# A graph network's attention decoder: one run of steps over all parts, with tanh, arguments and exponentials in one order, and sums in six tiles of one bank

## The chip, the cores and the metric

The kernel runs on one core of a Trainium2 chip. The metric is the device time of one execution, in microseconds (us); the time of a kernel is the median over its runs. The engines are named as the profile names them: PE is TensorE (its weight loads are PEld), DVE is VectorE, ACT is ScalarE, POOL is GpSimd, SP is SyncE, which here only issues transfers. Each engine works through its own list of instructions in order, and waits on semaphores for the others.

## The reference

Four graph layers over the same 2708 nodes with 512 features, each followed by a residual sum and a layer norm. Only the first matters here: an attention encoder, an mlp, and a decoder that uses the same attention again.

```python
sig = sigmoid(f1[:, :, None] + f2[:, None, :])         # heads x nodes x nodes
local_att = masked_softmax(local_pattern * sig, mask)  # both patterns are adj here
long_att = masked_softmax(long_range_pattern * sig, mask)
att = 0.5 * long_att + 0.5 * local_att
Xa = einsum('hij,hjd->hid', att, Xw)                   # encoder, 4 heads of 128
emb = mlp_block(batchnorm(Xa), ...)                    # h = elu(x W + b) + x, batchnorm
Y = einsum('hij,hjd->hid', att, emb by heads)          # decoder: the same attention
Y = elu(einsum('hnd,hed->hne', Y, W))
out = mlp_block(Y, ...)
x = layernorm(x + out)
```

The other layers are a mean over neighbours, and two attention layers with softmax over full score matrices. The change doesn't touch them.

## The kernel before

The decoder needs the exponentials of the attention again and has no room to keep them, so it forms most of them anew. Its sums are cut into four **parts**: half of the destination nodes (`hf`, 1354 columns each, in three chunks of at most 452) times a pair of heads (`p`). The order of the parts (`PARTS`) is (0,0), (0,1), (1,0), (1,1). A part has 22 **steps**, one for each block of 128 source nodes in `ORDER`; the block of the last 20 nodes, the remnant, stands at place 11. So there are 88 steps, in the text S0 to S87.

A step is either formed or kept. A **formed** step (`form`, L625) loads a block of the masked adjacency (`a`, 677 KB, SP's queue, three buffers), makes two tanhs on ACT, one for each head of the pair (`tanhs`, L383), multiplies with the mask on DVE (`arguments`, L378), and takes the exponential of both heads at once on ACT (L635). All of it works in place in a tile `t` of 128 x 2 x 1354 numbers, of which there are four buffers. DVE also counts each block's neighbours (`count`, L615), once for each half of the nodes: with the first formed step that has the block in hand. In a **kept** step, `t` is loaded back from DRAM (1354 KB), where the encoder wrote it: places 8, 11, 14 and 18 of the parts with p = 0, and places 1, 4, 7, 9, 11, 14, 17 and 20 of those with p = 1 (`KEPT`); the remnant at place 11 is kept in all four. Of the 88 steps 64 are formed and 24 kept.

Then come the **sums** (`feature_sums`, L640, matmul at L650): for the two heads and three chunks one matmul each into one of six PSUM sums `po`, which last for the whole part. The profile records each as two, so a full step has 12 records. The six sums lie in three tiles of two banks (`po0` to `po2`), used again by each part.

At the end of a part, `decode` (L1036) takes the sums: six times `take` (L1054, DVE) multiplies one sum with a scale and with the softmax's reciprocal sums `rb` into `ot`. Then, for each of the six, `shifted` (L1067, DVE), and `turn`: a matmul with the head's weights into `ps_y` (L1079) and elu (L699 on ACT, L706 and L708 on DVE). After the parts with p = 1 the decoder's mlp follows (`ps_dec`, L1093, elu at L701). This work isn't done at once: `decode` returns it as a list, `later`, and one piece is popped at each step of the next part (`later.pop(0)()`). The last part's is written out in `decode` itself. `rb` (L355, two loads of 677 KB) and a mask `linked` (L1041, DVE) are made at a part's start.

The order on an engine is that in which the program issues, unless a scheduler finds by its own estimates that another is better; `tc.issue_after(x)`, here wrapped as `behind(x)`, tells it that what is issued inside must stand behind x. Before, the decoder has only one such order for its work: a count stands behind its step's arguments. The rest, which tanh stands ahead of which exponential, is the scheduler's choice.

Ahead of the decoder stands the encoder's mlp (L954 to L985), in six chunks of nodes: four matmul groups of a chunk (`ps_mlp`, L964) into the same PSUM tiles `po0` to `po2`, two groups to a tile, elu, a sum and statistics on DVE, then transposes of the finished blocks (`tp_emb`, L983) and their copies to `emb` on ACT (L984). The decoder's first tanhs are made beside it.

The functions that the change touches:

Of the kernel before, what the change touches and what calls it, by code (L numbers as in the profile page):

```python
# [8 lines left out]
F32 = mybir.dt.float32  # L9
# [3 lines left out]
AF = mybir.ActivationFunctionType  # L13
# [4 lines left out]
P = 128  # L18
# [11 lines left out]
def gnn_stack_kernel(  # L30
# [25 lines left out]
    nc = tc.nc  # L56
    N, F = x.shape
    H = w0.shape[1]
    C = F // P
    NT = (N + P - 1) // P  # L60
    NFULL = N // P
    BLOCKS = [(i * P, min(P, N - i * P)) for i in range(NT)]
    BANK = 512


    Q = 32
# [71 lines left out]
    NHALF, HB, HP = 2, 3, 2  # L138
    HW = 2 * ((N + 3) // 4)
# [24 lines left out]
    ORDER = list(range(NT // 2)) + [NT - 1] + list(range(NT // 2, NT - 1))  # L164
# [5 lines left out]
    KEPT = [(8, 11, 14, 18), (1, 4, 7, 9, 11, 14, 17, 20)]  # L170
    KEPT = [[ORDER[k] for k in places] for places in KEPT]
# [17 lines left out]
    with ExitStack() as l0:  # L189
# [39 lines left out]
        def behind(*which):  # L229
            stack = ExitStack()  # L230
            for work in which:
                stack.enter_context(tc.issue_after(work.ins))
            return stack
# [116 lines left out]
        def spread_sums(att, hf, p):  # L350

            h0, w = HSPAN[hf]
            t = att.tile([P, HP, HW], F32, tag="rb", name="rb", bufs=1)
            for k in range(HP):
                nc.sync.dma_start(  # L355
                    t[:, k, :w], rs_d[HP * p + k, h0 : h0 + w].partition_broadcast(P)
                )
            return t
# [17 lines left out]
        def arguments(t, a, n, w):  # L376
            ab = a[:n, :w].unsqueeze(1).to_broadcast([n, HP, w])
            return nc.vector.scalar_tensor_tensor(t, t, GUARD, ab, ALU.add, ALU.mult)  # L378

        def tanhs(t, f1b, hf, p, jt, n, w):  # L380
            for k in range(HP):
                h = HP * p + k
                done = nc.scalar.activation(  # L383
                    t[:, k, :],
                    f1b[k][:n, :w],
                    AF.Tanh,
                    bias=f2h[:n, jt, h : h + 1],
                    scale=0.5,
                )
            return done  # L390
# [214 lines left out]
        def decoder_pass(values, att, psum, finish):  # L605

            def count(hf, jt, att, a=None):

                h0, w = HSPAN[hf]
                j0, n = BLOCKS[jt]  # L610
                if a is None:
                    a = att.tile([P, HW], F32, tag="a", name="a", bufs=3)
                    nc.sync.dma_start(a[:n, :w], adj_d[j0 : j0 + n, h0 : h0 + w])
                z = att.tile([P, HW], U8, tag="z", name="z", bufs=1)
                nc.vector.tensor_scalar(  # L615
                    z[:n, :w],
                    a[:n, :w],
                    -0.5 * BIG,
                    None,
                    ALU.is_lt,  # L620
                    ALU.add,
                    accum_out=zeros[:n, jt, hf : hf + 1],
                )

            def form(hf, p, jt, att, f1b, t, rows):  # L625

                h0, w = HSPAN[hf]
                j0, n = BLOCKS[jt]
                a = att.tile([P, HW], F32, tag="a", name="a", bufs=3)
                loads.append(nc.sync.dma_start(a[:n, :w], adj_d[j0 : j0 + n, h0 : h0 + w]))  # L630
                if n < P:
                    load_few(a, adj_d, h0, w)
                tanhs(t, f1b, hf, p, jt, rows, w)
                step = arguments(t, a, rows, w)
                nc.scalar.activation(t, t, AF.Exp, scale=0.5)  # L635
                if p == (jt in KEPT[0]):

                    with tc.issue_after(step.ins):
                        count(hf, jt, att, a)

            def feature_sums(part, place, t):

                hf, p = part
                jt = ORDER[place]
                n = BLOCKS[jt][1]
                for k in range(HP):
                    h = HP * p + k
                    for q, (q0, qw) in enumerate(HCH[hf]):
                        r = 0 if n == P else q * Q
                        nc.tensor.matmul(  # L650
                            po[HB * k + q][:, :qw],
                            values[r : r + n, jt, h * P : (h + 1) * P],
                            t[r : r + n, k, q0 : q0 + qw],
                            start=(place == 0),
                            stop=(place == NT - 1),
                        )

            later, loads = [], []
            for part in PARTS:
                hf, p = part  # L660
                h0, w = HSPAN[hf]
                for place, jt in enumerate(ORDER):
                    n = BLOCKS[jt][1]
                    if place == 0:
                        f1 = f1_d[HP * p : HP * (p + 1), h0 : h0 + w].partition_broadcast(P)
                        both = att.tile([P, HP, HW], F32, tag="f1b", name="f1b", bufs=2)
                        f1b = [both[:, k, :] for k in range(HP)]
                        with behind(*loads[-9:-8]):
                            nc.sync.dma_start(both[:, :, :w], f1)
                        rb = spread_sums(att, hf, p)  # L670
                    elif later:
                        later.pop(0)()
                    t = att.tile([P, HP, HW], F32, tag="t", name="t", bufs=4)
                    kept = kept_d.get((hf, p, jt))
                    if kept is None:
                        rows = n if n == P else HR
                        form(hf, p, jt, att, f1b, t[:rows, :, :w], rows)
                    else:
                        for r in range(0, P if n == P else HB * Q, P if n == P else Q):
                            nc.sync.dma_start(t[r : r + n, :, :w], kept[:n, :, :w])  # L680
                        if p == 0 and jt in KEPT[1]:
                            count(hf, jt, att)
                    if place == 0:
                        both = [
                            psum.tile([P, HP, BANK], F32, tag=f"po{q}", name="po", bufs=1)
                            for q in range(HB)
                        ]
                        po = [both[q][:, k, :] for k in range(HP) for q in range(HB)]
                    feature_sums(part, place, t)
                later += finish(hf, p, po, rb) or []  # L690
            for work in later:
                work()

# [216 lines left out]
        with (  # L910
# [43 lines left out]
            for ci, (c0, w) in enumerate(CHUNKS):  # L954
                if ci + 1 < NCH:
                    normal(ci + 1)
                pss = []
                for o in range(C):
                    if o % HP == 0:
                        slot = (C * ci + o) // HP % HB  # L960
                        pair = psum.tile([P, HP, BANK], F32, tag=f"po{slot}", name="ps_mlp")
                    ps = pair[:, o % HP, :]
                    for c in range(C):
                        nc.tensor.matmul(  # L964
                            ps[:, :w],
                            enc_w[:, c, o * P : (o + 1) * P],
                            ft[:, c, c0 : c0 + w],
                            start=(c == 0),
                            stop=(c == C - 1),
                        )  # L970
                    pss.append(ps)
                for o in range(C):
                    dst = ft[:, o, c0 : c0 + w]
                    r = elu(
                        att, pss[o][:, :w], w, prm_sb[:, MB_ENC, o : o + 1], less[:, o : o + 1]
                    )
                    nc.vector.tensor_tensor(dst, dst, r, ALU.add)
                    nc.vector.bn_stats(stats[:, o, ci, :], dst)
                while turned < NT and sum(BLOCKS[turned]) <= c0 + w:
                    j0, n = BLOCKS[turned]  # L980
                    tp = psum.tile([P, C, P], F32, tag="misc", name="tp_emb", bufs=2)
                    for c in range(C):
                        nc.tensor.transpose(tp[:n, c, :], ft[:, c, j0 : j0 + n], ident)  # L983
                    nc.scalar.copy(emb[:n, turned, :], tp[:n].rearrange("p c d -> p (c d)"))  # L984
                    turned += 1  # L985
# [1291 lines left out]
```

## Time and profile before

| what | value |
|---|---|
| median of three runs | 3121.74 us (3119.06 to 3122.14) |
| the profiled execution | 3120.7 us |
| its span in the trace, mean granted clock | 3118.8 us, 0.997 |
| busy: PE, DVE, ACT, POOL | 3070.6, 2025.3, 1353.1, 175.2 us |
| the decoder's sums, from first to last record | 589.57 to 1028.07 us |
| parts of the decoder, by the windows view | 590 to 695, 695 to 796, 796 to 905, 905 to 1028 us |
| encoder's mlp, PE busy in 505 to 590 | 83.35 us |
| after the decoder's sums, 1028 to 1176, PE busy | 145.87 us |

A time in the trace counts from the span's start. "Idle before" is the time for which an engine stood still just ahead of an instruction or a group of them, with the instruction that ended it ("<-ACT t L635"). Matmuls are pipelined: the end of a record is modelled, and within a run of matmuls it lies 0.17 us after the start of the next. The granted clock is a share of TensorE's full speed. All shares of busy time over the whole span mix four layers; what a change of the decoder is worth can only be read from its own windows.

### The profile page before, as it was taken

Reading aid. Unit: us, or ns where it says so; the run is one execution under the profiler, and the core shown is the slowest. Engines: PE = TensorE matmul, PEld = TensorE weight load, DVE = VectorE, ACT = ScalarE, POOL = GpSimd, SP = SyncE. Lnnn points to the kernel's source line nnn. Section 1 sums busy time; section 2 is a strip of 40 time slices with the busy share of each in tenths; the row PEclk is TensorE's granted clock in tenths of the full one; section 3 lists DMA queues with packets and bytes.
Section 4 is the critical chain, followed back from the end, with each engine's and each line's share of the span. In section 5 each row is a group of like instructions: output and inputs, shape, how many; then the busy total and the mean of one; then the engine's idle time right before and its main releaser. Section 6 shows DMA issues by size and latency. Waiting matters only on the chain.

```text
span 3118.8 us, 39610 instructions
## 1 busy us (share of the span) xinstructions
PE 3070.6 (98%) x15144; PEld 2336.9 (75%) x15144; DVE 2025.3 (65%) x3804; ACT 1353.1 (43%) x1655; POOL 175.2 (6%) x301
## 2 busy tenths in 40 slices
PE   8999999999999999999999999999999999999999
PEld 7999996544444447875588887787778888888886
DVE  7988966785885783452366668677555555555565
ACT  7999998587767350001133334435211111111111
POOL 1111100000000000000111101000010000000000
PEclk9999999999999999999999999999999999999999
DMA  8987964266445315530254445566331111111110
GB/s 277 333 313 251 321 235 144 79 232 221 161 173 192 108 42 158 144 97 31 67 166 133 136 138 165 164 177 184 108 95 36 50 51 51 51 51 50 50 52 29
DMA packets 207228, 430.10 MB, mean 138 GB/s; under 512 B 22218, under 2 KB 137598, under 8 KB 201294
## 3 DMA queue, kind: packets, MB, share of 16 engines
q1 hardware_dynamic: 182774, 326.20, 34.0%
q0 software_dynamic: 24256, 101.35, 8.9%
q8 instruction: 119, 1.95, 0.3%
q14 instruction: 71, 0.58, 0.1%
q10 hardware_dynamic: 8, 0.02, 0.0%
HBM read 330.07 MB, written 95.87 MB: 137 GB/s over the span
## 4 chain that ended last, share of the span: by engine, by line
PE 79%; ACT 8%; DVE 8%; issue 3%; DMA 1%; SPq 0%; DVEq 0%; ACTq 0%; POOLq 0%
PE po L1728 21%; PE ps_s L1523 18%; PE po L650 9%; PE ps_nb L1326 7%; PE ps_wide L1376 5%; PE po L548 4%; ACT t L383 4%; ACT t L515 3%; DVE t L378 2%; PE ps_v L131 2%; PE ps_sup L1934 2%; PE ps_hid L131 2%; PE ps_dec L1093 2%; PE ps_mlp L964 1%; DVE a L444 1%
## 5 line engine op out<-in xcount | busy, mean ns | idle before, releaser
L378 DVE SCALAR_TENSOR_TENSOR t<-t,a 128x2708 f32<-128x2708 f32 (+1 forms) x152 | 443.8, 2922 | 166.1 <-ACT t L383 165.8
L548 PE MATMUL po<-xw,t 128*128 128x129 f32 (+2 forms) x3872 | 428.2, 277 | 11.8 <-DVE rc L781 4.9
L548 PEld LDWEIGHTS po<-xw,t 128*128 128x128 f32 (+2 forms) x3872 | 422.8, 189 | 16.4 <-issue 7.9
L383 ACT ACTIVATE t<-f1b,f2h 128x1354 f32<-128x1354 f32 x296 | 404.4, 1412 | 34.2 <-PE po L650 34.2
L1523 PE MATMUL ps_s<-q,hT 128*128 128x256 f32 (+1 forms) x1848 | 405.5, 372 | 0.0
L1728 PE MATMUL po<-sup,e 128*128 128x256 f32 (+1 forms) x1512 | 398.2, 384 | 5.6 <-DVE c L1809 2.8
L650 PE MATMUL po<-t,emb 128*128 128x452 f32 (+3 forms) x1056 | 399.1, 547 | 4.3 <-ACT t L635 4.2
L1523 PEld LDWEIGHTS ps_s<-q,hT 128*128 128x128 f32 x1848 | 339.5, 190 | 49.5 <-issue 5.1
L650 PEld LDWEIGHTS po<-t,emb 128*128 128x128 f32 (+1 forms) x1056 | 194.2, 191 | 202.1 <-issue 189.2
L1728 PEld LDWEIGHTS po<-sup,e 128*128 128x128 f32 (+1 forms) x1512 | 264.7, 185 | 59.6 <-issue 19.8
L1728 PE MATMUL po<-held,T 128*128 128x256 f32 x1200 | 293.8, 380 | 0.0
L1728 PEld LDWEIGHTS po<-held,T 128*128 128x128 f32 x1200 | 227.0, 190 | 31.1 <-issue 0.9
L2129 DVE SCALAR_TENSOR_TENSOR e<-a_cols,ps_s 128x512 f32<-128x512 f32 (+1 forms) x121 | 79.6, 658 | 233.8 <-PE ps_s L1523 229.9
L1523 PE MATMUL ps_s<-hT 128*128 128x256 f32 (+2 forms) x968 | 213.8, 372 | 0.8 <-ACT sup L1941 0.7
L515 ACT ACTIVATE t<-t 128x2708 f32<-128x2708 f32 x88 | 209.2, 2377 | 8.8 <-DVE t L378 8.1
L1523 PEld LDWEIGHTS ps_s<-hT 128*128 128x128 f32 x968 | 175.1, 190 | 29.1 <-issue 3.9
L1326 PE MATMUL ps_nb<-hid_hi,at 128*128 128x512 f32 x484 | 185.6, 390 | 0.4 <-DVE at L1318 0.4
L635 ACT ACTIVATE t<-t 128x2708 f32<-128x2708 f32 x64 | 157.3, 2458 | 60.4 <-DVE t L378 60.2
L1326 PE MATMUL ps_nb<-hid_lo,at 128*128 128x512 f32 x462 | 180.0, 390 | 0.0
L2031 ACT ACTIVATE a_score<-a_score,neg_big 128x512 f32<-128x512 f32 (+3 forms) x131 | 88.4, 683 | 196.0 <-DMA a_score<-in_adjT_dram 98.9
L2121 ACT ACTIVATE q<-ps_wide,uq 128x256 f32<-128x256 f32 (+1 forms) x44 | 20.5, 465 | 335.7 <-PE ps_wide L1376 335.7
L1633 ACT ACTIVATE e<-e 128x512 f32<-128x512 f32 (+1 forms) x187 | 113.8, 615 | 118.2 <-DVE e L1632 117.9
(276 smaller groups left out, 3995.4 us busy)
## 6 DMA issues: line engine op xcount, KB each, us to landing
a<-adj_d SPq DMA_DIRECT2D x113, 677.0 KB
a_cols<-in_adjT_dram SPq DMA_DIRECT2D x200, 256.0 KB
kept<-t POOLq DMA_DIRECT2D x20, 1354.0 KB, 8.4
t<-kept SPq DMA_DIRECT2D x20, 1354.0 KB
raw<-in_adjT_dram SPq DMA_DIRECT2D x105, 256.0 KB
a<-in_adjT_dram SPq DMA_DIRECT2D x37, 677.0 KB
adj_d<-a POOLq DMA_DIRECT2D x37, 677.0 KB, 6.2
a_score<-in_adjT_dram SPq DMA_DIRECT2D x55, 256.0 KB
```

The costliest lines, as they stand in the source:

```text
L131: nc.tensor.matmul(ps[:n], xt[:, c, :n], w[:, c, :], start=(c == 0), stop=(c == C - 1))
L378: return nc.vector.scalar_tensor_tensor(t, t, GUARD, ab, ALU.add, ALU.mult)
L383: done = nc.scalar.activation(t[:, k, :], f1b[k][:n, :w], AF.Tanh, bias=f2h[:n, jt, h : h + 1], scale=0.5,)
L515: nc.scalar.activation(t, t, AF.Exp, scale=0.5)
L548: nc.tensor.matmul(po[k][b][:m, s * DR : (s + 1) * DR], t[own : own + n, k, i0 : i0 + m], values[own : own + n, jt, HP * p + k, :], start= ...
L635: nc.scalar.activation(t, t, AF.Exp, scale=0.5)
L650: nc.tensor.matmul(po[HB * k + q][:, :qw], values[r : r + n, jt, h * P : (h + 1) * P], t[r : r + n, k, q0 : q0 + qw], start=(place == 0), ...
L1326: nc.tensor.matmul(pos[it][:n], at, half[:, jt, :], start=(jt == 0 and k == 0), stop=(jt == NT - 1),)
L1376: nc.tensor.matmul(ps[:, :width], w(c, o), xt(c), start=(c == 0), stop=(c == C - 1),)
L1523: nc.tensor.matmul(ps[:, jb, i:w], keys[:, c, j : j + P], st["q"][:, c, i:], start=(c == 0), stop=(c == C - 1),)
L1633: return nc.scalar.activation(e, e, AF.Exp)
L1728: nc.tensor.matmul(po[bank][rows, half, :], lhsT, rhs, start=(k == 0 and half == 0) if first is None else first, stop=last, skip_group_che ...
```

## The change

Nothing is added to the work: each engine gets the same instructions as before, in another order, from the encoder's mlp on. Four things change.

1. The loop over parts and places becomes one loop over the 88 steps, in which `prepare(k)` runs two steps (`AFTER`) ahead of the sums: a part's first steps are prepared before the part ahead of it has issued its last sums and its `decode`.
2. Explicit orders: a step's tanhs stand behind the last exponential issued; its arguments behind the last arguments; the exponential of a formed step is issued only when the next formed step has issued its tanhs, and stands behind them; a count stands behind its step's arguments. So ACT gets tanh and exponential strictly in turn, over the kept steps too.
3. The six sums get a tile of one bank each, `po0` to `po5`, and so does `ps_mlp` in the encoder's mlp.
4. `rb` is loaded where a part's first sums are issued, behind the loads of `a` that were prepared ahead.

```diff
-            def form(hf, p, jt, att, f1b, t, rows):
+            def begin(hf, p, jt, f1b, t, rows):
...
                 loads.append(nc.sync.dma_start(a[:n, :w], adj_d[j0 : j0 + n, h0 : h0 + w]))
...
-                tanhs(t, f1b, hf, p, jt, rows, w)
-                step = arguments(t, a, rows, w)
-                nc.scalar.activation(t, t, AF.Exp, scale=0.5)
+                with behind(*exps[-1:]):
+                    tanh = tanhs(t, f1b, hf, p, jt, rows, w)
+                with behind(*args[-1:]):
+                    args.append(arguments(t, a, rows, w))
+                if open_exps:
+                    end(tanh)
+                open_exps.append(t)
                 if p == (jt in KEPT[0]):
-                    with tc.issue_after(step.ins):
+                    with behind(args[-1]):
                         count(hf, jt, att, a)
+
+            def end(*after):
+                t = open_exps.pop()
+                with behind(*after):
+                    exps.append(nc.scalar.activation(t, t, AF.Exp, scale=0.5))
...
-            for part in PARTS:
-                for place, jt in enumerate(ORDER):
...
+            AFTER = 2
+            def prepare(k):
+                (hf, p), place = STEPS[k]
...
+            state = {}
+            for k in range(len(STEPS) + AFTER):
+                if k < len(STEPS):
+                    prepare(k)
+                elif open_exps:
+                    end()
+                if k < AFTER:
+                    continue
+                part, place = STEPS[k - AFTER]
+                if place == 0:
+                    rb = spread_sums(att, *part)
+                    po = [
+                        psum.tile([P, BANK], F32, tag=f"po{b}", name="po", bufs=1)
+                        for b in range(HP * HB)
+                    ]
+                elif later:
+                    later.pop(0)()
+                feature_sums(part, place, tiles[k - AFTER])
+                if place == NT - 1:
+                    later += finish(*part, po, rb) or []
```

and in the encoder's mlp:

```diff
-                    if o % HP == 0:
-                        slot = (C * ci + o) // HP % HB
-                        pair = psum.tile([P, HP, BANK], F32, tag=f"po{slot}", name="ps_mlp")
-                    ps = pair[:, o % HP, :]
+                    slot = (C * ci + o) % (HP * HB)
+                    ps = psum.tile([P, BANK], F32, tag=f"po{slot}", name="ps_mlp")
```

More of the change, by code (lines that the diff above doesn't have):

```diff
@@ L656, in feature_sums @@
                         )
-            later, loads = [], []
-            for part in PARTS:
-                hf, p = part
+            later, loads, args, exps, open_exps, tiles = ([] for _ in range(6))
+            AFTER = 2
+            def prepare(k):
+                (hf, p), place = STEPS[k]
                 h0, w = HSPAN[hf]
-                for place, jt in enumerate(ORDER):
[L663 to L690, printed above, removed]
@@ new lines, in prepare @@
+                jt = ORDER[place]
+                n = BLOCKS[jt][1]
+                if place == 0:
+                    f1 = f1_d[HP * p : HP * (p + 1), h0 : h0 + w].partition_broadcast(P)
+                    f1b = att.tile([P, HP, HW], F32, tag="f1b", name="f1b", bufs=2)
+                    with behind(*loads[-9:-8]):
+                        nc.sync.dma_start(f1b[:, :, :w], f1)
+                    state["f1b"] = [f1b[:, i, :] for i in range(HP)]
+                t = att.tile([P, HP, HW], F32, tag="t", name="t", bufs=4)
@@ new lines, in prepare @@
+                kept = kept_d.get((hf, p, jt))
+                tiles.append(t)
+                if kept is None:
+                    rows = n if n == P else HR
+                    begin(hf, p, jt, state["f1b"], t[:rows, :, :w], rows)
+                    return
+                for r in range(0, P if n == P else HB * Q, P if n == P else Q):
+                    nc.sync.dma_start(t[r : r + n, :, :w], kept[:n, :, :w])
+                if p == 0 and jt in KEPT[1]:
+                    count(hf, jt, att)
@@ new lines, in decoder_pass @@
+            state = {}
[7 more added lines that the diff above has]
+                part, place = STEPS[k - AFTER]
+                if place == 0:
+                    rb = spread_sums(att, *part)
[8 more added lines that the diff above has]
+                    later += finish(*part, po, rb) or []
```

## The prediction, made before the changed kernel had run

> **What bounds it now.** I read the page's groups first, for the three lines of the decoder that the change reorders (line, engine, tiles, count, busy us, mean ns, then idle ahead of them and its releaser):
>
> ```profile
> L383 ACT ACTIVATE t<-f1b,f2h 128x1354 f32<-128x1354 f32 x296 | 404.4, 1412 | 34.2 <-PE po L650 34.2
> L650 PE MATMUL po<-t,emb 128*128 128x452 f32 (+3 forms) x1056 | 399.1, 547 | 4.3 <-ACT t L635 4.2
> L635 ACT ACTIVATE t<-t 128x2708 f32<-128x2708 f32 x64 | 157.3, 2458 | 60.4 <-DVE t L378 60.2
> ```
>
> ACT stood idle for 60 us ahead of the exponentials, but PE's sums lost 4.3 us in the whole decoder. Next the windows view over the decoder's four parts (PE, PEld, DVE, ACT, POOL busy, granted clock):
>
> ```profile
> 590.00:695.00 105.00, 104.03 (x291) 51.46 (x290) 79.38 (x71) 86.98 (x59) 1.56 (x3) 1.00 0.58 192
> ...
> 796.00:905.00 109.00, 108.53 (x285) 53.68 (x286) 95.89 (x101) 75.48 (x56) 0.00 (x0) 0.97 0.49 166
> 905.00:1028.00 123.00, 123.00 (x332) 61.05 (x331) 70.19 (x56) 85.36 (x54) 0.00 (x0) 1.00 0.49 175
> ```
>
> **PE bounds the decoder**: in the last part nothing is lost at all. What can be won is in PE's timeline, where its runs break (start, duration, count, idle ahead in brackets):
>
> ```profile
> 644.06 4.82 PE L650 MATMUL po<-t,emb 128*128 128x452 f32 x12 [0.27 <-ACT t L635]
> 649.04 36.67 PE L650 MATMUL po<-t,emb 128*128 128x452 f32 x96 [0.16 <-ACT t L635]
> ...
> 796.44 7.61 PE L650 MATMUL po<-t,emb 128*128 128x452 f32 x12 [3.30 <-ACT t L635]
> 803.89 0.92 PE L1079 MATMUL ps_y<-ot,w0T_sb 128*128 128x452 f32 x2
> 804.64 4.71 PE L650 MATMUL po<-t,emb 128*128 128x452 f32 x12
> ```
>
> I number the 88 steps S0 to S87 in PE's order; T, A and E are a step's tanh pair, arguments and exponential. Twelve records are one step: 4.71 us alone, and 36.67 us for eight, so (36.67 - 0.17)/8 = 4.56 from start to start (each record's end overlaps the next start by 0.17); I use 4.55. ACT's timeline beside it:
>
> ```profile
> 643.91 2.72 ACT L383 ACTIVATE t<-f1b,f2h 128x1354 f32<-128x1354 f32 x2
> 646.54 2.44 ACT L635 ACTIVATE t<-t 128x2708 f32<-128x2708 f32 x1
> 648.97 2.74 ACT L383 ACTIVATE t<-f1b,f2h 128x1354 f32<-128x1354 f32 x2
> ```
>
> 643.91 to 648.97 is a tanh pair and an exponential: 5.05 us, more than PE's 4.55. ACT keeps up only through the 24 kept steps, which it need not form.
>
> **Removed.** The break at S44 is the largest: 3.30 us idle, then twelve records in 7.61 instead of 4.71 us, 6.2 us in all. Its E44 stood behind tanhs of later steps. In the built kernel's lists of each engine's instructions E43 and E44 come earlier, with about 4 us of slack: removed. Four breaks of the first two parts (S6, S12, S13, S21; idle 0.16 to 0.43, each plus 0.17 of overlap and 0.1 for the restart) make 2.0 us, one at S50 0.3. **Sum removed: 8.5 us.** If E44 were late all the same, they shrink to 2.3.
>
> **Added: the exponential behind a kept step.** The new order puts E(k) behind the tanh of the next formed step. Where that is k+1, its buffer (four there are) was freed by S(k-3), long ago. Where k+1 is a kept step, the next formed one is k+2, and its tanh needs the buffer that S(k-2) still reads. So: S(k-2) ends 0.17 after S(k-1) starts; the tanh follows 0.09 later (653.86 to 653.95 in the trace); then 2.66 of tanhs, 2.46 of exponential, 0.06 until PE starts (648.98 to 649.04). That is 5.44 us from the start of S(k-1) to that of S(k), where PE needs 4.55: late by 0.89, with the restart 1.0. The lists put such a pair at T9/E7, T12/E10, T15/E13, T19/E17 in the first part, 32/30, 34/32, 37/35, 40/38, 43/41 in the second, 63/61 in the third and five in the fourth. Not every one costs 1.0:
>
> - First part: E3 no longer stands in the mlp phase. Behind the table load (T at 600.86) come two tanhs and a copy, 1.33 + 0.47 + 1.31, then E3 until 606.43, so S3 starts at 606.49 for 605.13 before: 1.46 with the restart. ACT has then no lead, and S4 to S7 run at ACT's 5.03 instead of 4.55: 2.0 together. S10, S13, S17: 1.0 each. Sum 6.5.
> - Second part: S30, S32, S35, S38, S41: 5.1.
> - Third part: S61, 1.0.
> - Fourth part: five holes, into which the lists put one matmul of the decoder's mlp each (0.757 us, one of four that take 3.03); 0.23 is left of each, 1.2.
>
> A gain is excluded: nothing starts earlier by standing behind more. **Sum 13.8 us.** If I have the release of the buffers wrong and E(k) finds room, it is 0 to 3.
>
> **Added: the seam into the third part.** DVE's timeline of before:
>
> ```profile
> 793.83 3.65 DVE L1054 SCALAR_TENSOR_TENSOR ot<-po,bn_scale,rb 128x452 f32<-128x452 f32 x6
> 797.40 0.68 DVE L1067 SCALAR_TENSOR_TENSOR ot<-ot,bn_shift,linked 128x452 f32<-128x452 f32 x1
> 798.00 1.55 DVE L615 TENSOR_SCALAR_CACHE_REDUCE z<-a 128x1354 uint8<-128x1354 f32 x1
> ...
> 800.08 2.97 DVE L378 SCALAR_TENSOR_TENSOR t<-t,a 128x2708 f32<-128x2708 f32 x1
> ...
> 806.52 0.68 DVE L1067 SCALAR_TENSOR_TENSOR ot<-ot,bn_shift,linked 128x450 f32<-128x450 f32 x1
> ```
>
> The first shift (L1067), which ps_y's first matmul (L1079) needs, follows the takes at once. In the new lists A46, its count, A47 and its count (2.9 + 1.57, twice) stand between them. With S41's start as zero: T45 ends at 7.67, A45 and its count at 12.1, the takes at 15.8, A46 and count at 20.3, A47 and count at 24.7, the shift at 25.3 (each by the rows above). PE asks for it after S44, S45 and one matmul of S46: 13.7 + 9.1 + 0.76 = 23.55. PE is in order, so the rest of S46 waits behind: 1.95 with the restart. Each later shift follows a full DVE step: args 2.9, count 1.57, shift 0.6, and elu's two operations 0.54 each, 6.15 us, against 4.55 + 0.76 = 5.3 on PE: 0.8 to 1.25 late four times more, until the sixth. **Sum 5.75 us**; at least 0, if DVE starts the takes 2 us earlier and the sum of a step hides it, at most 5 x 0.85 + 1.95 + two clock drops.
>
> Such a drop is in the trace: the clock of 796:800 was 0.50 after the idle 3.30 us. A gap of 2.07 us (263.83) was followed by a half clock too, one of 1.91 (1088.5) was not. A wait of 1.95 lies between; half speed for 3.41 us costs 1.7 at most. I take 0 and keep 1.7 in the range. [...]
>
> **Costed at nothing.** The six one-bank tiles: no break of PE in the decoder has a take (L1054) as releaser; a bank could be asked for earlier only if one had. The mlp loop's banks: its breaks are the transposes waiting for DVE's ft, 3.8 us in all, not for a free pair; bounds -3.8 and +1.5, and I take 0, since a freed bank doesn't speed DVE. The loads of rb stand on SP behind three loads of 677 KB instead of ahead, which at the 260 GB/s of 262:266 is 7.8 us: rb landed at 507.7, now near 515. Behind it on DVE waits the first elu of the mlp; PE's first transposes waited 1.1 us there before and about 1.0 by the new order. Without that cover, DVE would be late by 7.8 us, and PE by what its mlp matmuls don't hide, 1.5 or so. Kept loads one load later on SP (2.6 us) land many us ahead of their steps. The tail has the same operations: 0, give or take 1.5.
>
> **The sum.** 13.8 + 5.75 - 8.5 = +11.1. The profiled execution took 3120.7 us (span 3118.8): 3131.8, and the median of the runs shown is 1.0 above that execution. I forecast **3132 us**.
>
> **Rivals.**
> - **The waits behind kept steps alone.** DVE gets the takes earlier than I reckon, and the shifts come in time: 13.8 - 8.5 = +5.3, 3126. For it: DVE's window at 796 holds 95.89 of 109 us, so there is room; against: the order is strict, and the counts stand ahead.
> - **The gains alone: faster.** ACT's average has room in each part: the first has 18 formed steps of 5.03, 90.5 us, and PE's 21 full steps take 95.6. If ACT, freed of its 58.6 us of waits for arguments, runs a step ahead of PE, then every E(k) is done before PE asks, and only the removal is left: -8.5, 3112. It decides in its favour if the tanh of k+2 finds its buffer free, that is if T(k+2) to E(k) fits into 4.55 us from the release; by the rows it takes 5.18, before any latency. That speaks against.
> - **Nothing.** The waits and the gains cancel, or the sums don't move as PE's chain swallows them: 3121.
> - **Worse.** Two or three of the waits reach the half clock (1.7 each), the mlp is late by 1.5 and the tail too: +11.1 + 5 + 3, some 3142 at the far end.
>
> **How the numbers follow.** Forecast 0.55 at 3132 (own range 3126 to 3139); kept-step waits alone 0.15 at 3126, of which some lies within 0.2%; gains alone 0.12; nothing 0.08; worse 0.10. The range 3119 to 3142 leaves out the gains and little else. 0.2%, 6.2 us, is about what a measurement of this kernel tells from no change. Faster by more: 0.12. Within: nothing's 0.08, the 3126 case's 0.15 and a little of the forecast, 0.25. Slower: 0.63.
>
> **What would show it.** PE's timeline: no idle at S44; breaks of about 0.7 us before S10, S13, S17, S30, S32, S35, S38, S41 with ACT's exponential as releaser; near S46 a ps_y matmul that waits about 1.8 us for DVE's shift, four more of about 0.8. ACT's timeline: tanh and exponential in strict turn, with waits of tanh for PE. It would be wrong if PE has no breaks behind kept steps, if the shift is there before S46, or if PE's mlp phase ends elsewhere than 589.6.

## The result, and the profile after

The changed kernel takes 3127.62 us (median of nine runs, 3125.15 to 3131.09), the kernel before beside it 3120.66 us (3115.26 to 3122.14): a ratio of 1.0025, 95% interval 1.0015 to 1.0034, which is 4.7 to 10.6 us slower. The prediction was +11.1 us; the two profiled spans differ by 7.4 us (3126.2 against 3118.8).

The same three groups of the page as before:

```profile
L383 ACT ACTIVATE t<-f1b,f2h 128x1354 f32<-128x1354 f32 x296 | 404.9, 1413 | 89.9 <-PE po L660 89.4
...
L660 PE MATMUL po<-t,emb 128*128 128x452 f32 (+3 forms) x1056 | 399.3, 545 | 5.7 <-ACT t L649 5.7
...
L649 ACT ACTIVATE t<-t 128x2708 f32<-128x2708 f32 x64 | 156.7, 2448 | 6.9 <-DVE t L378 6.9
```

ACT's idle time has changed its place: ahead of the exponentials 60.4 us have become 6.9, ahead of the tanhs 34.2 have become 89.9, and those wait for PE. The exponentials no longer wait for their arguments; they stand behind a tanh that waits for a buffer.

PE's timeline of the changed kernel, second part (S30 to S44):

```profile
734.87 9.37 PE L660 MATMUL po<-t,emb 128*128 128x452 f32 x24 [0.69 <-ACT t L649]
744.92 11.28 PE L660 MATMUL po<-t,emb 128*128 128x452 f32 x36 [0.69 <-ACT t L649]
756.66 13.91 PE L660 MATMUL po<-t,emb 128*128 128x452 f32 x36 [0.46 <-ACT t L649]
771.21 13.91 PE L660 MATMUL po<-t,emb 128*128 128x452 f32 x36 [0.63 <-ACT t L649]
785.75 14.67 PE L660 MATMUL po<-t,emb 128*128 128x452 f32 x38 [0.63 <-ACT t L649]
```

These are S30, S32, S35, S38 and S41, whose exponentials stand behind the tanh of a step beyond a kept one. S25 and S28 do so too, but there PE has a turn of 0.757 us more to do at each step, and isn't late; S22 is late by 0.1 us. The seam into the third part, PE's timeline:

```profile
810.87 1.78 PE L1101 MATMUL ps_y<-ot,w0T_sb 128*128 128x452 f32 x4 [1.34 <-DVE ot L1089]
812.49 4.71 PE L660 MATMUL po<-t,emb 128*128 128x452 f32 x12
818.05 1.02 PE L1101 MATMUL ps_y<-ot,w0T_sb 128*128 128x450 f32 x2 [0.85 <-DVE ot L1089]
818.91 4.71 PE L660 MATMUL po<-t,emb 128*128 128x452 f32 x12
824.10 1.03 PE L1101 MATMUL ps_y<-ot,w0T_sb 128*128 128x452 f32 x2 [0.47 <-DVE ot L1089]
```

The idle of 3.30 us at S44 is gone, and the matmuls that turn a sum (L1101; L1079 in the kernel before) wait for DVE's shift instead. DVE beside it:

```profile
797.82 3.66 DVE L1076 SCALAR_TENSOR_TENSOR ot<-po,bn_scale,rb 128x452 f32<-128x452 f32 x6
801.39 2.97 DVE L378 SCALAR_TENSOR_TENSOR t<-t,a 128x2708 f32<-128x2708 f32 x1
...
805.76 2.97 DVE L378 SCALAR_TENSOR_TENSOR t<-t,a 128x2708 f32<-128x2708 f32 x1
...
810.13 1.28 DVE L1089 SCALAR_TENSOR_TENSOR ot<-ot,bn_shift,linked 128x452 f32<-128x452 f32 x2
```

Between takes and first shift stand two steps of arguments and counts, 797.82 + 3.6 to 810.13.

Where 7.3 of the 7.4 us between the two traces lie, by the starts of PE's records (intervals between the same two records in both):

| stretch | before | after | difference |
|---|---|---|---|
| up to the work ahead of the encoder's mlp, not touched | 489.44 | 490.15 | +0.7 |
| encoder's mlp | 84.47 | 83.94 | -0.5 |
| S0 to S22 | 101.34 | 103.95 | +2.6, of which 0.76 is a ps_y matmul moved ahead of S22 |
| S22 to S43 | 97.51 | 101.23 | +3.7, in spite of the 0.76 |
| S43 to S65 | 132.92 | 132.16 | -0.8 |
| S65 to S87 | 102.18 | 106.66 | +4.5, of which 3.8 are five matmuls of the decoder's mlp (0.757 each) moved forward |
| S87 to the first matmul of layer 1 | 67.09 | 63.11 | -4.0, the same 3.8 given back |
| the rest, not touched | 2022.1 | 2023.1 | +1.0 |

So the decoder with its tail costs some 6 us (2.6 + 3.7 - 0.8 + 4.5 - 4.0); of the rest, 1.7 us lie in stretches that the change doesn't touch.

### The profile page after: what moved, and what is told of

Read it like the earlier page. It is cut to its first block, busy times and chain, and to the rows that moved or that the text cites. A ratio compares the mean times of both kernels' runs of the same rounds, so it can differ in the third digit from the quotient of the medians.

```text
span 3126.2 us, 39640 instructions
## 1 busy us (share of the span) xinstructions
PE 3073.1 (98%) x15144; PEld 2334.5 (75%) x15144; DVE 2025.9 (65%) x3804; ACT 1350.8 (43%) x1655; POOL 175.2 (6%) x301
## 4 chain that ended last, share of the span: by engine, by line
PE 81%; ACT 9%; DVE 6%; issue 2%; DMA 1%; POOL 0%; SPq 0%; DVEq 0%; ACTq 0%; POOLq 0%
PE po L1750 21%; PE ps_s L1545 19%; PE po L660 9%; PE ps_nb L1348 7%; PE po L548 5%; PE ps_wide L1398 5%; ACT t L383 4%; ACT t L515 3%; PE ps_v L131 2%; PE ps_sup L1956 2%; PE ps_dec L1115 2%; PE ps_hid L131 2%; DVE t L378 1%; ACT t L649 1%; PE ps_mlp L986 1%
## 5 line engine op out<-in xcount | busy, mean ns | idle before, releaser
L383 ACT ACTIVATE t<-f1b,f2h 128x1354 f32<-128x1354 f32 x296 | 404.9, 1413 | 89.9 <-PE po L660 89.4
```

Source lines behind the costliest of these rows:

```text
L383: done = nc.scalar.activation(t[:, k, :], f1b[k][:n, :w], AF.Tanh, bias=f2h[:n, jt, h : h + 1], scale=0.5,)
```

## The experiments

The two theories of the prediction, the wait behind kept steps (an exponential behind a tanh that needs a late buffer) and the shifts behind two steps of DVE's work, were each taken away alone, then both. Each time stands beside runs of the kernel before on the same chip.

**The exponential ahead of kept steps** (`exp_first`), on the changed kernel:

```diff
                 tiles.append(t)
+                if kept is not None and open_exps:
+                    end()
                 if kept is None:
```

> The changed kernel, with one more line: where the next step is a kept one, the last formed step's exponential is issued before it, so ahead of the next tanh instead of behind it. Theory (the chain buffer free, tanh, exponential makes the breaks): PE's breaks at S10, S13, S17, S30, S32, S35, S38, S41 and S61, 0.67 to 0.96 us each and 7.7 us together in the changed kernel's trace, go, and with them the 0.7 us around the five matmuls put into the fourth part; the waits for the shifts at S46 to S50 (4.95 us) stay. The kernel is 7 to 8.5 us faster than the changed one, about 3119.5. Rival (ACT's load of 5.0 us a formed step is the bound, whatever the order): the breaks move to other steps, and less than 2 us are won.

Measured: 3118.41 us, 0.9994 of before (0.9985 to 1.0003); the changed kernel stood at 1.0025, so 0.0031 or 9.7 us less, somewhat more than expected and within the intervals. Its PE timeline for the second part is one line where the changed kernel had five breaks:

```profile
733.70 66.52 PE L660 MATMUL po<-t,emb 128*128 128x450 f32 x182
```

The breaks behind kept steps are gone, and few came in their place. In the first part S5 and S6 are late by 0.17 and 0.43 us as in the changed kernel, and where that one had S16 and S17 late (0.18 and 0.67), here it is S15 and S16 (0.57 and 0.43). The waits at the seam of the third part remain (4.6 us with restarts, for 4.9). In the fourth part S65 to S87 takes 101.99 us, 4.67 less, of which 3.79 are the matmuls that go back to the tail: the five holes cost 0.9 us beyond what filled them.

**The shifts two pieces ahead** (`shift2`), on the changed kernel:

```diff
-                def after(k, q):
-                    shifted(k, q)
-                    turn(k, q)
+                def ahead(heads, i):
+                    if i + 2 < len(heads):
+                        shifted(*heads[i + 2])
+                    turn(*heads[i])
...
-                    rest = [lambda k=k, q=q: after(k, q) for k in range(HP) for q in range(HB)]
+                    heads = [(k, q) for k in range(HP) for q in range(HB)]
+                    for head in heads[:2]:
+                        shifted(*head)
+                    rest = [lambda i=i: ahead(heads, i) for i in range(HP * HB)]
```

> The changed kernel, with the shifts issued two pieces ahead of the matmul that needs them: the first two straight behind the takes, each later one with the matmul two before its own. Theory (the shift stands on DVE behind two steps of arguments and counts, and PE in order waits for it): the five waits of ps_y in the third part, 1.6 + 1.1 + 3 x 0.74 = 4.95 us with restarts, go; 4 to 5 us faster than the changed kernel, about 3122.7. The breaks behind kept steps stay. Rival (DVE, with 6.15 us of work a step there against 5.3 on PE, is the bound): the arguments come late in place of the shifts, ACT's exponentials with them, and PE loses 2 to 4 us at S46 to S52 instead.

Measured: 3123.51 us, 1.0009 of before (1.0001 to 1.0018): 5.0 us less than the changed kernel by the ratios. Of the five waits one of 0.15 us (and 0.1 of restart) is left, at the sixth turn. S43 to S65 shrank by 4.5 us, and the other stretches of the decoder kept their lengths to 0.01 us.

**Both** (`both2`):

> Both edits: the exponential ahead of kept steps, and the shifts two pieces ahead. If both theories hold and the two costs are independent: 12 to 13.5 us faster than the changed kernel, about 3115, and so 5 to 7 us faster than before: what remains is the gain of the change, the break of 6.2 us at S44 that is gone. If either rival holds, it is not faster than before by more than 2 us.

Measured: 3113.62 us, 0.9978 of before (0.9969 to 0.9987), 6.9 us faster than before and 14.7 less than the changed kernel by the ratios, which is the sum of the two single edits (9.7 + 5.0). Within their intervals the costs add up, and what remains is the gain that the change had.

**The tiles alone** (`banks_alone`): the kernel before, with the six one-bank tiles for the decoder's sums and the mlp's, as the change's diff has them.

> The kernel before, with nothing but the six one-bank tiles, for the decoder's sums and for the encoder's mlp. Theory: no wait in the decoder has a take as its releaser, so the decoder gains nothing, the break of 6.2 us at S44 stays, and the mlp gains at most the 0.5 us that its traces differ by: within 2 us of before. Rival: the banks, not the order, removed the break at S44 or cost something in the mlp: 4 us or more of difference either way.

Measured: 3119.7 us, 0.9999 of before (0.999 to 1.0008): the time as expected, the reason not. The break at S44 did not stay; its PE timeline:

```profile
785.76 8.51 PE L650 MATMUL po<-t,emb 128*128 128x450 f32 x22
794.94 4.06 PE L650 MATMUL po<-t,emb 128*128 128x452 f32 x10 [0.68 <-DVE ot L1051]
```

Two records of S44 run without a wait, then PE waits 0.68 us for a take (L1051 here), and the granted clock stays at 1.00 (794 to 802). So S44 had not waited for the exponential that the profile named: its counterpart starts only at 794.32 here, behind S44's first record at 793.34. ACT's timeline of the kernel before, which I had read too quickly, agrees:

```profile
787.14 2.44 ACT L635 ACTIVATE t<-t 128x2708 f32<-128x2708 f32 x1
789.49 4.04 ACT L383 ACTIVATE t<-f1b,f2h 128x1354 f32<-128x1354 f32 x3
793.95 2.46 ACT L635 ACTIVATE t<-t 128x2708 f32<-128x2708 f32 x1 [0.41 <-DVE t L378]
```

By ACT's list the exponential at 787.14 is E44, done at 789.58: it is the 33rd of the 64, and 32 formed steps stand ahead of S44. The one at 793.95 is E45; the one behind it ends at 808.29, too late for S45 at 804.64. What ended S44's wait at 796.44 was the fourth take, whose end the trace has at 796.29: the pair of banks that S44's first matmul writes holds sums 1 and 4. E45 ended at 796.41 by chance, and the profile named it, being the last. What the tiles gain here, they lose elsewhere: with the list that the scheduler makes for them, S13 breaks by 2.2 us for 0.3 before, and S46 to S50 by 0.5 to 0.7 each (one at S50 was all that stood there before).

**The takes ahead** (`takes_first`): the kernel before, with one order more.

```diff
-                step = arguments(t, a, rows, w)
+                with behind(*took if (hf, p) == (1, 0) and jt == ORDER[1] else []):
+                    step = arguments(t, a, rows, w)
```

`took` holds the last take that was issued.

> The kernel before, with one order more: the arguments of the third part's second step (S45) stand behind the last take of the second part. Nothing else is changed, neither the tiles nor the exponentials' place. Theory (S44 waited for the takes, not for an exponential): S44 starts within 0.3 us of S43's end, and there is no half clock behind it; the arguments of S45 and its exponential come 3 us later, and the shifts move with them, which may cost 1 to 2 us again at the next steps: 4 to 6 us faster than before. Rival (S44 waited for an exponential, as the profile's releaser says): the break stays at 3 us or more, and the time is that of before or worse.

Measured: 3120.35 us, 1.0002 of before (0.9993 to 1.0011). The break at S44 is gone but for 0.1 us, which tells takes from exponential. (The takes of a pair of banks now also come one behind the other: the second take ends at 792.20, S44 starts at 792.35.) The time is not won, though, since the next wait takes its place. PE's timeline:

```profile
783.51 13.82 PE L653 MATMUL po<-t,emb 128*128 128x452 f32 x35
797.17 0.92 PE L1082 MATMUL ps_y<-ot,w0T_sb 128*128 128x452 f32 x2
800.20 1.80 PE L1082 MATMUL ps_y<-ot,w0T_sb 128*128 128x452 f32 x2 [2.11 <-DVE ot L1070]
```

The list now has two turns behind S44, and the second shift stands behind S45's arguments and count: 2.27 us, then some 3.4 us at half the clock (0.57 granted on average over 800 to 804), and 1.1 us more at a later turn. The expected 4 to 6 us missed.

**The order alone** (`order_alone`): the changed kernel with pairs of banks.

```diff
-                    po = [
-                        psum.tile([P, BANK], F32, tag=f"po{b}", name="po", bufs=1)
-                        for b in range(HP * HB)
-                    ]
+                    both = [
+                        psum.tile([P, HP, BANK], F32, tag=f"po{q}", name="po", bufs=1)
+                        for q in range(HB)
+                    ]
+                    po = [both[q][:, i, :] for i in range(HP) for q in range(HB)]
```

and the mlp's pairs as before.

> The changed kernel with the order of the steps as it is, but the sums of decoder and mlp in three tiles of two banks, as before. The prediction has the 6.2 us at S44 removed by the order of the exponentials; the run with the banks alone, where that break shrank to 0.84 us with the old order, speaks for the takes. Theory now: before, S44 waited for the fourth take of the pair of banks, and the takes stood on DVE behind the arguments of S45, which waited for a tanh. The new order puts the takes ahead of any waiting arguments (they start at 797.82 in the changed kernel); with pairs, S44 needs the fourth, at about 800.3, and is asked for at 799.5: a break of 0.8 to 1.0 us with a take as the late one, 1 us slower than the changed kernel, 3128 to 3129. Rival (the order of the exponentials removed the break, the banks are nothing): no break at S44, same time as the changed kernel.

Measured: 3140.25 us, 1.0067 of before (1.0054 to 1.0079). Both expectations missed: S44 has no break, and two new ones stand at S22 and S66. PE's timeline, then DVE's, at the first of them:

```profile
697.96 6.48 PE L660 MATMUL po<-t,emb 128*128 128x452 f32 x12 [3.83 <-DVE ot L1079]
```

```profile
692.44 2.98 DVE L378 SCALAR_TENSOR_TENSOR t<-t,a 128x2708 f32<-128x2708 f32 x1 [5.69 <-ACT t L383]
695.34 3.66 DVE L1079 SCALAR_TENSOR_TENSOR ot<-po,bn_scale,rb 128x452 f32<-128x452 f32 x6
```

It is the old S44 again, at two other seams: the scheduler puts the takes behind the arguments of a step whose tanh waits (5.69 us), and PE waits for the fourth take (it ends at 697.81) and then takes 6.48 us for twelve records instead of 4.71. At S44 its takes come in the order of the pairs, and two of them free the first: S44 is late by 0.1 us.

The run is not the tiles alone, though, for DVE's list changed with them. In the changed kernel, with six tiles, the takes at this seam start at 689.29 and stand ahead of the arguments:

```profile
690.62 3.15 DVE L1076 SCALAR_TENSOR_TENSOR ot<-po,bn_scale,rb 128x452 f32<-128x452 f32 x5
693.68 5.86 DVE L378 SCALAR_TENSOR_TENSOR t<-t,a 128x2708 f32<-128x2708 f32 x2
```

The kernel before has pairs, and its takes ahead too (from 689.48), and there S22 is late by no more than 0.1 us. So pairs cost this much only together with the place of the takes. How much of it six tiles would save with DVE's list as it is here was not run; the first take ends at 696.03, the fourth 1.8 us later.

**Both edits, with pairs** (`both2_pairs`):

> The version with both edits (the exponential ahead of kept steps, shifts two pieces ahead), with the sums in three pairs of banks. If the one-bank tiles are worth something only where a take is late: about 1 us at S44, and up to 1 us more at the other two seams, so 1 to 3 us slower than the version with six tiles. If they are worth nothing: the same.

Measured: 3129.03 us, 1.0028 of before (1.0017 to 1.0038), so 15.6 us more than with six tiles: the breaks at S22 (late by 5.75 us) and S66 (late by 3.93) are there, S44 is late by 0.17, and the profiled execution's mean granted clock is 0.996, for 0.998 with six tiles. At S22 the profile names an exponential again (it ends at 698.24), and again by ACT's list it is a later one: E22, the 19th, ended at 690.11, and the fourth take at 698.13, ahead of S22 at 698.28. The expected 1 to 3 us were far too little.

**Five buffers of t** (`buf5_f1`): the changed kernel, order untouched, with `bufs=5` for t and `bufs=1` for f1b.

> The changed kernel with five buffers of t instead of four; to make room, the tile f1b has one buffer instead of two, so a part's first tanh waits for the f1b load after the last tanh of the part ahead, and the seams are disturbed (some us at S22, S44, S66). Inside the parts: if the break behind a kept step comes from the buffer that the next tanh waits for, it goes (S30, S32, S35, S38, S41, S61: under 0.2 us each) though the order is the same. If it comes from the order alone (tanh and exponential one behind the other are too long), the breaks stay at 0.6 to 0.9 us.

Measured in a single run: 3117.42 us. All breaks behind kept steps are gone, those of the first part too: its PE timeline has all from 609.57 to 694.67, past the first seam, in one line, and the third part is left with the shifts:

```profile
609.57 85.10 PE L660 MATMUL po<-t,emb 128*128 128x452 f32 x231
...
802.93 1.78 PE L1101 MATMUL ps_y<-ot,w0T_sb 128*128 128x452 f32 x4 [2.89 <-DVE ot L1089]
```

The order by itself is harmless; with four buffers it makes the exponential wait for a buffer that it doesn't need. PE shows no break at the seams, against what I had expected of the single f1b, though ACT waits 4.86 us for f1b's load at the first of them.

**Five buffers and the shifts** (`buf5_shift`), **and the exponentials too** (`buf5_both`):

> The changed kernel with five buffers of t (f1b one) and the shifts two pieces ahead; the exponentials stay behind the next tanh. The breaks behind kept steps are gone with the fifth buffer, the waits of ps_y in the third part (5.2 us in the one look at five buffers) go with the shifts: no break over 0.2 us in the decoder but one at the third seam's end, about 3112, some 8 us faster than before. If the shifts' wait turns into late exponentials, about 3115.

> As the one before, with the exponential ahead of kept steps too. If the buffer and the order are two cures of one and the same wait, nothing is added: the same time within 1.5 us. If the order costs something of its own (a tanh delayed by the exponential ahead of it, or the reverse), they differ by 2 us or more.

Measured: 3112.53 us, 0.9975 of before (0.9966 to 0.9984), and 3114.65 us, 0.9981 (0.9973 to 0.999). The first has the lowest median of all, 7.8 us below before by its ratio, though its interval overlaps that of both edits with four buffers; in its decoder two breaks are left, of 0.40 and 0.81 us, at the end of the third part's turns. The second has one more, 1.65 us at S21, and the medians differ by 2.1 us, more than the 1.5 expected, though their intervals overlap. The traces tell why: E21 stands behind the first tanh of the next part, and that waits for f1b. With the exponentials ahead, the last tanh that reads the single f1b ends at 671.89 instead of 669.17, f1b is loaded at 673.02 instead of 669.20, and E21 ends at 685.30, S21 starting at 685.35. So nothing is gained by curing the wait twice, and with one buffer of f1b something is lost; with two it was not run.

## Why the prediction was right where it was, and wrong where it was

**The direction and the two mechanisms held.** The added waits measure 15.0 us where 19.6 were reckoned (idle and restart together); with the 8.5 us of breaks taken off, that is 6.5 for 11.1, and the medians differ by 7.0:

| term | reckoned | measured |
|---|---|---|
| first part, S3 to S7 | 3.5 | 1.2 |
| first part, S10, S13, S16, S17 | 3.0 | 2.6 |
| second part, five breaks | 5.1 | 4.4 |
| third part, S61 | 1.0 | 1.0 |
| third part, five waits for shifts | 5.75 | 4.9 |
| fourth part, beyond what fills the holes | 1.2 | 0.9 |

**The step that failed in size is the start of the first part**: "Behind the table load (T at 600.86) come two tanhs and a copy". I left the table load (1.28 us in both traces) where it was. ACT's timeline before, then after:

```profile
594.70 1.43 ACT L383 ACTIVATE t<-f1b,f2h 128x1354 f32<-128x1354 f32 x1 [3.30 <-PE po L650]
```

```profile
598.96 1.43 ACT L383 ACTIVATE t<-f1b,f2h 128x1354 f32<-128x1354 f32 x1
...
600.75 1.42 ACT L383 ACTIVATE t<-f1b,f2h 128x1354 f32<-128x1354 f32 x1
602.08 2.44 ACT L649 ACTIVATE t<-t 128x2708 f32<-128x2708 f32 x1
```

The half of a tanh pair that stood at 594.70 before, where it held the copies and the table loads behind a wait for PE, left that stretch, and all of it came 1.9 us earlier (598.96 for 600.86), so E3 ended at 604.5, before S3 asked at 605.3, and S4 had no wait either: 2.3 us of the difference. When an instruction is moved, what stood behind it moves too. The other terms behind kept steps are up to 0.3 high at each break: breaks add up to 0.72 (S35) to 0.96 instead of 1.0. The waits for shifts were reckoned 0.85 too high together.

**The step that failed in cause**: "Its E44 stood behind tanhs of later steps". The 6.2 us went, as forecast, but they had been the takes', behind arguments that waited for a tanh, and the pair of banks; two runs (the tiles alone, the takes ahead) and the trace's own times of E44 show it. With it falls "The six one-bank tiles: no break of PE in the decoder has a take (L1054) as releaser". By the label none had; the largest one was a take's. In the new order the tiles, with the list of DVE that comes with them, are worth 13 us (3140.25 against 3127.62), in the old one 0. So it was luck that costing them at nothing did no harm: had the same change come without the tiles, my reckoning would have been the same and 9 us off. The small breaks at S12, S21 and S50 went as said (the four of 2.0 us together all lie in the first part). S13 breaks now behind a kept step, and S6, whose idle was 0.10 before and not 0.16 or more, breaks again, with S5 and S7, where ACT's exponentials are 4.98 us apart; S16 breaks too.

**Costed at nothing**: the mlp gained 0.5 us, inside its bounds; rb, the kept loads and the tail cost nothing that shows. **The clock** held after the longest wait, 1.34 us, as taken (1.00 granted in 806 to 818).

**The rivals.** "The gains alone" was to be decided by whether a tanh beyond a kept step finds its buffer free. It didn't, and the run with five buffers shows that this was the point: there it does, and the time is on the other side of before (3117.42 in a single run; 3112.53 with the shifts ahead). The rival with kept-step waits alone (3126) lies nearer to 3127.62 than the forecast, but its reason, shifts in time, is false: their waits are in the trace.

## What to carry to other kernels

A forced order "this behind that" costs nothing while the instruction put ahead can run, and the whole wait where it can't (here 0.46 to 0.69 us of PE's idle at each of five steps with four buffers of t, none with five): for every pair, look up what buffer the leading one needs and who frees it. A releaser in a profile is the semaphore event that came last, so check that it is the right instance (which step's exponential?) before a cause is built on it, above all where a second engine finishes close by (at S44 before, the take at 796.29 and the exponential that was named at 796.41). A tile that spans two banks was freed by the later of its two readers (S44 before: the fourth take ended at 796.29, S44 began at 796.44); whether that matters depends on where those readers stand in their engine's list, and a change of the tiles can change that list too, so compare it before a difference is put down to the tiles.

## What the runs showed of the hardware

The length of a gap alone doesn't tell whether the clock falls: behind an idle of 2.11 us (the run with the takes ahead) PE ran at half the clock, behind one of 2.89 us (five buffers) it did not. The windows view has it (stretch, its length, PE's busy time; PE's granted clock is third from the end), first the takes ahead, whose gap ends at 800.20, then five buffers, whose gap ends at 802.93:

```profile
796.00:800.00 4.00, 2.09 (x6) 0.75 (x4) 4.00 (x4) 2.57 (x3) 0.00 (x0) 1.00 0.91 326
800.00:804.00 4.00, 3.80 (x6) 1.68 (x7) 4.00 (x4) 3.60 (x4) 0.00 (x0) 0.57 0.55 173
```

```profile
798.00:802.00 4.00, 2.04 (x6) 0.74 (x4) 4.00 (x2) 4.00 (x4) 0.00 (x0) 1.00 0.89 299
802.00:806.00 4.00, 3.07 (x8) 1.62 (x9) 4.00 (x5) 3.70 (x4) 0.00 (x0) 1.00 0.57 177
806.00:810.00 4.00, 4.00 (x11) 1.70 (x9) 4.00 (x8) 4.00 (x3) 0.00 (x0) 1.00 0.17 24
```

So the prediction's reading of the rows, a limit between 1.91 and 2.07 us on the length of a gap, is wrong. What else decides, these rows don't show.

Nor did the half clock always last as long as the prediction takes. In the kernel before it held for 3.41 us behind the gap of 2.07, and for 6.8 at S44, where it began within the gap of 3.30:

```profile
266.25:269.66 3.41, 3.41 (x18) 3.41 (x18) 3.41 (x19) 3.41 (x2) 0.00 (x0) 0.50 0.67 203
...
795.34:802.15 6.81, 5.71 (x8) 2.83 (x9) 6.81 (x9) 3.69 (x3) 0.00 (x0) 0.50 0.55 166
```

S44's twelve records took 7.61 us there instead of 4.71: 2.9 us lost, where the prediction has 1.7 at most for such a drop.
